# A deformable convolution's eviction issued behind the next band's first sample copy, and a second PSUM bank for split bands

## The chip, the cores and the metric

The kernel runs on one core of one Trainium2 chip. The time is device microseconds of one execution, here the median of several; lower is better. TensorE (PE) multiplies into PSUM[...]; ScalarE (ACT) and VectorE (DVE) read PSUM and write SBUF; GpSimd (POOL) and SyncE (SP) mostly issue transfers. Each engine works through its own instructions in order, and engines wait for one another by semaphores.

## The reference, cut to what matters

Input x has 8 images of 128 channels of 64 x 64 in fp32. Layer 0 is a group norm, a modulated deformable 3 x 3 convolution, a batch norm with ReLU, and the sum with x. Layer 1 is a group norm and a routed mixture of four 3 x 3 expert convolutions plus a shared one. The change lies in layer 0's deformable convolution:

```
om = conv3x3(x, off_w) + off_b            # 27 maps: y and x offsets, mask
off = om[:, :18].reshape(B, 9, 2, H, W);  mask = sigmoid(om[:, 18:])
py = off[:, :, 0] + rows + ky;  px = off[:, :, 1] + cols + kx
val = corner(y0, x0, (1 - ly) * (1 - lx)) + ... (four corners)
val = val * mask
out = einsum('bckhw,ock->bohw', val, w) + b
```

## The kernel before, in words

`dense()` computes layer 0 up to its statistics, with fp32 throughout; `layer1()` does the rest. Sampling is a product: for a tile of pixels, a matrix of bilinear weights (`s`, built by VectorE from the tables `x_wts` and `y_wts`, L868) is multiplied with the tile's input pixels (`xt`) on PE.

**Bands.** An image is eight bands of eight rows (`NB = 8`), 64 bands in all. The loop over g has 65 steps. Step g issues, in this order: for q = 0 to 4, `sample(5g+q)` (twelve PE products at L884 into one tile `pq`, then a ScalarE copy at L894 into `samples[g % 2]`) and `weights` of five groups later; behind q = 1, `put_off()`, which runs VectorE work set aside in `late`; and then `conv(g-1)`, the nine taps over the band before (L934, each tap two PE passes into `py`), with other work issued between the taps: the transposes of the pixels of band g+2 (L825 into `pt`, copied out at L828), the spreading and sharing of that band's tables (L776, L782, L841), loads (L738, L757), and pieces of the offset convolution of a later image (`tables`, L456 into `pc`). "The step j" below is the step whose samples are for the j-th band of an image, so that its convolution is for band j-1; the step j = 0 has the convolution of the last band of the image before.

**The convolution's output.** Behind its last tap, L942 evicts `py` with a bias into `y` on ScalarE, the batch norm's statistics of `y` go into `late` (L943, run at L1014), and L944 stores `y` from SP's queue. `py` has one bank (`ps_y`). A band covers 7 rows for j = 0 and 8 for j = 1 to 6; the last band of an image has two spans of 5 and 4 rows (320 and 256 columns), one behind the other in the same bank, each with its own nine taps, eviction and store.

**PSUM.** `ps_q` has three tiles of two banks (`pq`), so that the fourth group of a step waits for the copy of the first, and the fifth for that of the second. `ps_y` has one bank. `ps_c` has one bank under the tag `pc`, shared by the offset blocks and the transposes.

**What sets the order.** It is written out by hand: each engine runs its instructions in the order in which the Python code issues them (`manual_schedule`). The loads of tables go through POOL, the stores of `y`, of the offset maps and some copies through SP.

Of the kernel before, what the change touches and what calls it, by code (L numbers as in the profile page):

```python
# [8 lines left out]
F32 = mybir.dt.float32  # L9
I32 = mybir.dt.int32  # L10
AF = mybir.ActivationFunctionType
# [5 lines left out]
P = 128  # L17
# [5 lines left out]
CH = 512  # L23
# [42 lines left out]
def deform_moe_conv(  # L66
# [18 lines left out]
    nc = tc.nc  # L85
# [10 lines left out]
        out=gsel, in_=gsel, compare_op=ALU.is_ge, fill=0.0, base=0,  # L96
# [83 lines left out]
    def dense():  # L180

        with ExitStack() as st:
# [83 lines left out]
            count_f = a1.tile([1, 1], F32, name="count_f")  # L266

            nc.scalar.activation(count_f, nhalf[0:1], AF.Sigmoid)
            xts, ss, late = {}, {}, []
            bands = [(b, j) for b in range(B) for j in range(NB)]  # L270

            def pause(n):
# [527 lines left out]
            def pixels(g, turn_odd=False):  # L800

                if g >= len(bands):
                    return
                xts[g] = a2.tile([P, NCOL, P], F32, name="xt")
                if turn_odd:
                    for side in range(2):
                        nc.vector.tensor_copy(
                            picked_odd[:, :, :, T * side : T * side + T].rearrange(
                                "p c h x y -> p c h (x y)"
                            ),  # L810
                            picked[
                                :, 1 - side : EVEN - side, :, T * side : T * side + T
                            ].rearrange("p c h x y -> p c h (x y)"),
                        )
                for c0 in range(0, NCOL if turn_odd else EVEN, 4):
                    n = min(4, NCOL - c0)
                    if turn_odd:
                        pt = ps_q.tile([P, 2, CH], F32, name="pq")[:, 0].rearrange(
                            "p (c n) -> p c n", n=P
                        )  # L820
                    else:
                        pt = ps_c.tile([P, 4, P], F32, name="pt", tag="pc")
                    for c in range(c0, c0 + n):
                        one = picked[:, c] if c < EVEN else picked_odd[:, c - EVEN]
                        nc.tensor.transpose(  # L825
                            pt[:, c - c0], one.rearrange("p h x y -> p (h x y)"), ident
                        )
                    (nc.vector.tensor_copy if turn_odd else nc.scalar.copy)(  # L828
                        xts[g][:, c0 : c0 + n], pt[:, 0:n]
                    )  # L830
                    yield
# [90 lines left out]
            def conv(g):  # L922

                b, j = bands[g]
                o = 2 * T * j - 1
                spans = (
                    [(0, 7)] if j == 0 else [(o, 8)] if j < NB - 1 else [(o, 5), (o + 5, 4)]
                )
                for e, (o, n) in enumerate(spans):
                    py = ps_y.tile([P, CH], F32, name="py")[:, 0 : n * W]  # L930
                    for i in range(TAPS):
                        yy, xx = divmod(i, 3)
                        m = 3 * (o + 1 - yy - 2 * T * j + 2) + yy
                        nc.tensor.matmul(  # L934
                            py,
                            lhsT=dw_sb[:, 3 * (2 - yy) + 2 - xx],
                            rhs=samples[g % 2][:, m : m + 3 * n - 2 : 3, xx, 1 : W + 1],
                            start=(i == 0), stop=(i == TAPS - 1),
                        )
                        yield  # L940
                    y = a3.tile([P, CH], F32, name="y")[:, 0 : n * W]
                    nc.scalar.activation(y, py, AF.Identity, bias=db_sb)  # L942
                    late.append((nc.vector.bn_stats, ystats[:, b, j + e, :], y))  # L943
                    nc.sync.dma_start(out=ydram[b][:, o * W : (o + n) * W], in_=y)  # L944

            made, later = tables(0), tables(1)
            for q in range(4):
# [75 lines left out]
            for g in range(len(bands) + 1):  # L1023
                b, j = bands[g] if g < len(bands) else (B, 0)
                if j == NB - 4:
                    means_of = statistics(b + 2)
                turned = pixels(g + 2)
                if j == NB - 2:
                    tick()
                for q in range(NGR):  # L1030
                    if g < len(bands):
                        sample(g * NGR + q)
                        if g:
                            weights(g * NGR + q + AHEAD)
                        if g == 0 and q == 2:
                            for k in range(Q):
                                load_y(2, k, nc.gpsimd)
                    if g == 0 and q == 1:
                        for _ in range(4):
                            next(later)  # L1040
                    if q == 1:
                        put_off()
                taps = conv(g - 1) if g else iter(())
                twice = 2 if g and bands[g - 1][1] == NB - 1 else 1
                for done, _ in enumerate(taps):
                    part, odd = divmod(done, twice)
                    if odd == 0 and part in PIXELS:
                        next(turned, None)
                    if odd == 0 and part == 2:
                        load_x(g + 3, nc.gpsimd)  # L1050
                        if g < len(bands):
                            edges(g)
                    if odd == 0 and part > 6:
                        for k in range(T * (part - 7), T * (part - 6)):
                            load_y(g + 3, k, nc.gpsimd)
                    if odd == 0 and part in SPREAD:
                        step, half = divmod(SPREAD.index(part), 2)
                        if step:
                            spread(g + 2, HALVES[half], ())
                        else:  # L1060
                            spread(g + 2, sides_=(half,), clip=False)
                    if odd == 0 and part in SHARE:
                        piece = SHARE.index(part)
                        share(g + 2, piece, MOVES[piece])
                    if odd == 0 and j == NB - 4 and 0 < part < 7:
                        next(means_of, None)
                    if odd == 0 and j == NB - 3 and part == 0:
                        for _ in range(2):
                            next(means_of, None)
                    if odd == 0 and j == NB - 3 and part == 4 and b + 2 < B:  # L1070
                        for _ in made:
                            pass
                        asked, made = True, tables(b + 2)
                        next(made)
                    if odd == 0 and part in BLOCKS and asked:
                        asked = False
                        tick()
                    for _ in range(3 + (g < NB) if twice == 1 else 1 + done % 2):
                        tick()
                    if odd == 0 and part == 4:  # L1080
                        pick(g + 3)
                        if 2 <= j < 5:
                            load_quarter(b + 2, j - 1)
                    if odd == 0 and part == 8 and j == 1:
                        load_quarter(b + 2, 0)
                if g == 0:
                    edges(0)
                    spread(1)
                    for n in range(AHEAD):
                        weights(NGR + n)  # L1090
                for _ in turned:
                    pass
                if g == 0:
                    for piece in range(4):
                        share(2, piece, MOVES[piece])
                    load_x(3, nc.gpsimd)
                    for k in range(Q):
                        load_y(3, k, nc.gpsimd)
                    pick(3)
                    spread(2)  # L1100
                if g == 3:
                    quad_weights()
                if j < NB - 1 and g < len(bands):
                    late.append((hand_on, g))
                xts.pop(g - 1, None)
                if j == 1 and b:
                    nc.vector.bn_aggr(ymvs[:, b - 1], ystats[:, b - 1])
                if (b, j) == (B - 1, 1):
                    reach()
# [596 lines left out]
```

## Time and profile before

| | us |
|---|---|
| median of 3 runs (lowest to highest) | 1424.83 (1418.2 to 1427.55) |
| the profiled execution: its time, its span | 1419.31, 1417.3 |
| PE busy | 1290.2 (91%) |
| VectorE busy | 1063.5 (75%) |
| ScalarE busy | 834.3 (59%) |
| GpSimd busy | 477.6 (34%) |
| TensorE clock granted, mean | 0.967 of full |

A row of the profile gives source line, engine, operation, what is written and read, and how often, then busy time, mean ns of one, and the engine's idle time just ahead with what ended it. In a timeline a row begins with start and length; neighbouring instructions of one kind are merged into a row, with their number behind the x, and idle time ahead stands in brackets. Products on PE are pipelined, and their ends are modelled.

### The profile page before, as it was taken

How to read it: one execution, taken by the hardware profiler on the slowest of the kernel's cores; microseconds unless marked ns; L12 is line 12 of the kernel's file. 1: busy time of each engine (PE TensorE's matmuls, PEld its weight loads, DVE VectorE, ACT ScalarE, POOL GpSimd, SP SyncE). 2: the span in 40 equal slices, each digit the busy share in tenths (PEclk: the TensorE clock that was granted, in tenths of full speed). 3: DMA queues.
4: the chain of work that ended last, by engine and by line, in shares of the span. 5: the costliest groups of instructions: out<-in, count | busy, mean ns of one | idle time of the engine just before them, and what ended most of it. 6: DMA issues, size and time to landing. Idle time of an engine off the chain costs nothing.

```text
span 1417.3 us, 21259 instructions
## 1 busy us (share of the span) xinstructions
PE 1290.2 (91%) x7561; PEld 731.6 (52%) x7561; DVE 1063.5 (75%) x2124; ACT 834.3 (59%) x1110; POOL 477.6 (34%) x748
## 2 busy tenths in 40 slices
PE   4169889999999999999999999999948999999998
PEld 1144456555656655655565565666623444444443
DVE  5757868689788878968978886756448987778972
ACT  2365856886787688688679768767522333222220
POOL 6444044534425543452552554354021010001000
PEclk9579989999999999999999999999978999999999
DMA  4589686977978887897887887799245654456411
GB/s 145 114 192 206 137 182 157 213 182 171 210 181 180 194 195 175 180 207 184 193 210 183 179 207 159 159 228 220 66 160 147 163 146 123 127 153 178 104 57 51
DMA packets 149430, 234.55 MB, mean 165 GB/s; under 512 B 101677, under 2 KB 104890, under 8 KB 139074
## 3 DMA queue, kind: packets, MB, share of 16 engines
q0 software_dynamic: 79248, 136.19, 44.4%
q1 hardware_dynamic: 69522, 96.37, 24.2%
q8 instruction: 61, 1.00, 0.3%
q10 hardware_dynamic: 544, 0.54, 0.1%
q14 instruction: 55, 0.45, 0.1%
HBM read 180.23 MB, written 45.35 MB: 159 GB/s over the span
## 4 chain that ended last, share of the span: by engine, by line
PE 57%; DMA 12%; ACT 12%; issue 8%; DVE 6%; POOL 3%; SPq 2%; DVEq 0%; ACTq 0%; POOLq 0%
PE py L934 21%; PE pc L1618 17%; PE pq L884 11%; DMA ywts<-taby 3%; PE pc L456 3%; PE pt L825 3%; ACT xwts L776 2%; DMA combo<-colwise 2%; ACT work L638 2%; DMA pad<-in_x_dram 1%; ACT samples L894 1%; DMA x<-in_x_dram 1%; DVE s L868 1%; POOL ywts L738 1%; ACT xt L841 1%
## 5 line engine op out<-in xcount | busy, mean ns | idle before, releaser
L934 PE MATMUL py<-samples,dw_sb 128*128 128x512 f32 (+3 forms) x1296 | 555.1, 561 | 9.7 <-ACT y L942 9.7
L738 POOL DMA_DIRECT2D ywts<-taby x510 | 335.0, 671 | 368.0 <-DMA xwts<-tabx 151.8
L934 PEld LDWEIGHTS py<-samples,dw_sb 128*128 128x128 f32 x1296 | 226.8, 189 | 206.8 <-issue 174.2
L884 PE MATMUL pq<-s,xt 64*128 64x144 f32 (+1 forms) x3840 | 284.4, 302 | 29.8 <-ACT samples L894 22.5
L884 PEld LDWEIGHTS pq<-s,xt 64*128 64x128 f32 x3840 | 257.6, 191 | 78.6 <-ACT samples L894 26.9
L894 ACT COPY samples<-pq 128x864 f32<-128x864 f32 (+1 forms) x318 | 278.5, 973 | 27.2 <-PE pq L884 27.1
L868 DVE TENSOR_TENSOR s<-xwts,ywts 128x432 f32<-128x432 f32 (+1 forms) x448 | 199.0, 498 | 49.5 <-PE pq L884 45.4
L1618 PE MATMUL pc<-v,u 128*128 128x512 f32 x384 | 174.3, 600 | 6.3 <-DVE v L1525 6.3
L1618 PE MATMUL pc<-v,wmix 128*128 128x512 f32 x384 | 173.2, 596 | 0.0
L776 ACT ACTIVATE xwts<-xwts,place 128x1152 f32<-128x1152 f32 (+3 forms) x132 | 153.1, 1164 | 7.9 <-DMA xwts<-tabx 7.9
L782 DVE TENSOR_SCALAR xwts<-xwts 128x1152 f32<-128x1152 f32 (+2 forms) x128 | 96.0, 751 | 80.4 <-ACT xwts L776 75.3
L1596 ACT ACTIVATE t<-pc,bmix 128x512 f32<-128x512 f32 x32 | 22.0, 687 | 187.5 <-PE pc L1618 98.8
L757 POOL DMA_DIRECT2D xwts<-tabx x126 | 73.5, 590 | 164.3 <-DVE samples L911 34.9
L1618 PEld LDWEIGHTS pc<-v,u 128*128 128x128 f32 x384 | 71.8, 191 | 92.9 <-issue 83.1
L1618 PEld LDWEIGHTS pc<-v,wmix 128*128 128x128 f32 x384 | 72.0, 189 | 90.9 <-issue 88.9
L942 ACT ACTIVATE y<-py,db_sb 128x512 f32<-128x512 f32 (+3 forms) x72 | 45.8, 636 | 118.0 <-PE py L934 110.8
L828 ACT COPY xt<-pt 128x512 f32<-128x512 f32 x126 | 73.9, 587 | 61.0 <-PE pt L825 51.4
L825 PEld LDWEIGHTS pt<-ident,picked 128*128 128x128 f32 x504 | 59.0, 142 | 92.5 <-ACT xt L828 41.8
L825 PE MATMUL pt<-ident,picked 128*128 128x128 f32 x504 | 78.1, 278 | 23.5 <-DVE picked L791 17.0
L791 DVE COPY picked<-pad 128x512 f32<-128x512 f32 x128 | 71.9, 604 | 32.0 <-PE pt L825 31.9
L841 DVE COPY xt<-xt 32x896 f32<-32x896 f32 x126 | 77.7, 616 | 2.4 <-ACT xt L828 0.9
L1014 DVE BATCH_NORM_STATS2 ystats<-y 128x6 f32<-128x512 f32 (+3 forms) x72 | 44.2, 622 | 23.7 <-ACT y L942 23.7
(209 smaller groups left out, 1167.0 us busy)
## 6 DMA issues: line engine op xcount, KB each, us to landing
xwts<-tabx POOLq DMA_DIRECT2D x126, 576.0 KB, 8.5
pad<-in_x_dram SPq DMA_DIRECT2D x36, 512.0 KB
ywts<-taby POOLq DMA_DIRECT2D x126, 144.0 KB, 9.2
out_dram<-yo SPq DMA_DIRECT2D x32, 512.0 KB
ywts<-taby POOLq DMA_DIRECT2D x126, 108.0 KB, 8.9
yd<-y SPq DMA_DIRECT2D x48, 256.0 KB
ywts<-taby POOLq DMA_DIRECT2D x126, 72.0 KB, 8.3
pad<-yd SPq DMA_DIRECT2D x16, 512.0 KB
```

Of the source, the lines that this page charges most:

```text
L738: engine.dma_start(out=y_wts[g % 3][HALF * h + k : HALF * (h + n) : Q, first : last + 1].rearrange("p r a b c -> p (r a b c)"), in_=bass.A ...
L757: engine.dma_start(out=x_wts[g % 3][HALF * h : HALF * h + HALF], in_=bass.AP(tensor=x_table[b].tensor, offset=x_table[b].offset + (2 * j + ...
L776: nc.scalar.activation(some, some, AF.Abs, bias=columns[side])
L782: nc.vector.tensor_scalar(some, some, -1.0, 0.0, ALU.add, ALU.min)
L825: nc.tensor.transpose(pt[:, c - c0], one.rearrange("p h x y -> p (h x y)"), ident)
L828: (nc.vector.tensor_copy if turn_odd else nc.scalar.copy)(xts[g][:, c0 : c0 + n], pt[:, 0:n])
L841: move(out=xts[g][rows, EVEN:].rearrange("p c n -> p (c n)"), in_=xts[g][rows, 1 - side : EVEN - side].rearrange("p c n -> p (c n)"),)
L868: nc.vector.tensor_tensor(s[:, :, 3 * at : 3 * (at + k)].rearrange("p m (c x) -> p m c x", x=3), by_x[:, :, c : c + k], by_y[:, :, w : w + ...
L884: nc.tensor.matmul(by_m[:, h, :, at : at + k], lhsT=xts[g][rows, c // 2 + EVEN * (c % 2)], rhs=s[rows, :, at : at + k], start=True, stop=True,
L894: (nc.scalar.copy if g or q < 3 else nc.vector.tensor_copy)(bass.AP(tensor=one.tensor, offset=one.offset + first, ap=[list(one.ap[0]), [M ...
L934: nc.tensor.matmul(py, lhsT=dw_sb[:, 3 * (2 - yy) + 2 - xx], rhs=samples[g % 2][:, m : m + 3 * n - 2 : 3, xx, 1 : W + 1], start=(i == 0), ...
L1618: nc.tensor.matmul(pc, lhsT=us[j][:, kx], rhs=vs[g][:, rows, kx : kx + W], start=(kx == 0), stop=(kx == 2),)
```

## The change

Two edits of the convolution's output. First, the eviction with its statistics and its store is wrapped in a function `move`. For a band with one span it isn't run at once but put in the list `waiting`, and run in the next step of the loop behind `sample` of q = 0, that is behind the first sample copy in ScalarE's order (in the loop's last step, which has no samples, at its start). For a band with two spans it is run at once, as before. Second, the second span of such a band accumulates in the bank of `ps_c` instead of that of `ps_y`. The lists of instructions of the engines keep their lengths: on ScalarE each unsplit eviction stands one place later (in the steps j = 6 of the first images a normalisation also stands between), on VectorE its statistics follow the copy of four rows to the next band (L918, `hand_on`) instead of preceding it, and SP's order is unchanged.

```diff
@@ def conv(g)
                 for e, (o, n) in enumerate(spans):
-                    py = ps_y.tile([P, CH], F32, name="py")[:, 0 : n * W]
+                    if e == 0:
+                        py = ps_y.tile([P, CH], F32, name="py")[:, 0 : n * W]
+                    else:
+                        py = ps_c.tile([P, CH], F32, name="py2", tag="pc")[:, 0 : n * W]
...
-                    y = a3.tile([P, CH], F32, name="y")[:, 0 : n * W]
-                    nc.scalar.activation(y, py, AF.Identity, bias=db_sb)
-                    late.append((nc.vector.bn_stats, ystats[:, b, j + e, :], y))
-                    nc.sync.dma_start(out=ydram[b][:, o * W : (o + n) * W], in_=y)
+
+                    def move(e=e, o=o, n=n, py=py):
+                        y = a3.tile([P, CH], F32, name="y")[:, 0 : n * W]
+                        nc.scalar.activation(y, py, AF.Identity, bias=db_sb)
+                        late.append((nc.vector.bn_stats, ystats[:, b, j + e, :], y))
+                        nc.sync.dma_start(out=ydram[b][:, o * W : (o + n) * W], in_=y)
+
+                    if len(spans) > 1:
+                        move()
+                    else:
+                        waiting.append(move)
@@ the loop over g
                 turned = pixels(g + 2)
+                if g == len(bands) and waiting:
+                    waiting.pop()()
...
                     if g < len(bands):
                         sample(g * NGR + q)
+                        if waiting:
+                            waiting.pop()()
                         if g:
                             weights(g * NGR + q + AHEAD)
```

More of the change, by code (lines that the diff above doesn't have):

```diff
@@ L268, in dense @@
             nc.scalar.activation(count_f, nhalf[0:1], AF.Sigmoid)
-            xts, ss, late = {}, {}, []
+            xts, ss, late, waiting = {}, {}, [], []
             bands = [(b, j) for b in range(B) for j in range(NB)]
```

## The prediction

> **What bounds the kernel now.** I read the page's costliest groups first, then what TensorE (PE) waited for in one whole image, then busy time band by band, then the timeline of two bands. A band's step g runs five groups of sample products (L884), each copied out of PSUM by ScalarE (L894), and then the nine taps of the convolution of band g-1 (L934), evicted by L942. The page first:
>
> ```profile
> L934 PE MATMUL py<-samples,dw_sb 128*128 128x512 f32 (+3 forms) x1296 | 555.1, 561 | 9.7 <-ACT y L942 9.7
> L894 ACT COPY samples<-pq 128x864 f32<-128x864 f32 (+1 forms) x318 | 278.5, 973 | 27.2 <-PE pq L884 27.1
> L942 ACT ACTIVATE y<-py,db_sb 128x512 f32<-128x512 f32 (+3 forms) x72 | 45.8, 636 | 118.0 <-PE py L934 110.8
> ```
>
> ScalarE waits 110.8 us in all for the convolution to end: where it does, the eviction lies in an idle hole. PE waits 9.7 us for that eviction. PE's waits within one image (step 456.26 to 574.56), then its steps with the bands j = 3, 4 and 5 (columns: length, then busy us of PE, PE's loads, DVE, ACT):
>
> ```profile
> PE pq L884 <- ACT samples L894: 1.7, 2, 1.2
> PE py L934 <- ACT y L942: 0.9, 1, 0.9
> ...
> 502.70:515.82 13.12, 13.12 (x88) 7.88 (x87) 8.41 (x21) 11.33 (x16) 6.54 (x10) 1.00 1.07 213
> 515.82:529.78 13.96, 13.44 (x87) 7.97 (x87) 12.61 (x27) 13.45 (x19) 1.26 (x2) 1.00 0.74 187
> 529.78:544.87 15.09, 13.88 (x91) 8.42 (x91) 14.92 (x33) 11.59 (x16) 1.34 (x2) 1.00 0.79 180
> ```
>
> PE is busy in all of j = 3 at full clock; only j = 4 and 5 hold it up for ScalarE's copies, and j = 0 for the eviction. So PE's order of work is the time, and a stall added to a full band is added to the span. The timeline of the start of j = 3 (ScalarE ahead), of j = 4 (ScalarE behind), and of the end of j = 0's step:
>
> ```profile
> 502.70 4.21 PE L884 MATMUL pq<-s,xt 64*128 64x216 f32 x60
> 502.80 0.69 ACT L942 ACTIVATE y<-py,db_sb 128x512 f32<-128x512 f32 x1 [2.11 <-PE py L934]
> 503.87 4.40 ACT L894 COPY samples<-pq 128x1008 f32<-128x1008 f32 x5 [0.38 <-PE pq L884]
> 504.81 0.91 ACT L894 COPY samples<-pq 128x864 f32<-128x864 f32 x1
> ...
> 517.30 0.67 ACT L942 ACTIVATE y<-py,db_sb 128x512 f32<-128x512 f32 x1
> 517.87 4.31 ACT L894 COPY samples<-pq 128x1008 f32<-128x1008 f32 x5
> 518.94 1.94 PE L884 MATMUL pq<-s,xt 64*128 64x144 f32 x24 [0.52 <-ACT samples L894]
> ...
> 589.95 0.94 ACT L841 COPY xt<-xt 32x896 f32<-32x896 f32 x1
> 590.91 0.53 ACT L942 ACTIVATE y<-py,db_sb 128x320 f32<-128x320 f32 x1
> 591.49 4.22 PE L934 MATMUL py<-samples,dw_sb 128*128 128x256 f32 x18 [0.93 <-ACT y L942]
> ```
>
> In j = 3 the eviction runs from 502.80 to 503.49, while PE makes the first group; the first copy can't start before 503.87 anyway. It is free there. In j = 4 it is what the first copy waits for.
>
> **Part 1: the eviction behind the first copy.** Nothing is removed; 55 of the 72 evictions move (the sixteen of the split bands don't, and the last unsplit one has no copy to move behind). The products write three buffers of two banks, so group 4 waits for copy 1 and group 5 for copy 2. From the single records of j = 3, the groups start at 502.70, 503.66, 504.40, 505.13 and 505.87, and copy 2 ends at 504.81 + 0.91 = 505.72: 0.15 us before group 5 wants its buffer. With the move, copy 1 stays at 503.87, the eviction takes the place at 504.81, and copy 2 shifts by what an eviction takes from its start to the next start: 517.87 - 517.30 = 0.57. Copy 2 then ends at 506.29, group 5 starts 0.57 - 0.15 = 0.42 late, plus 0.02 to 0.09 to set off again (in j = 4 copy 1 is 0.88 later than in j = 3, measured from the step's start, with slack of 0.21 and 0.15 before groups 4 and 5, and the five groups take 0.84 longer). I take 0.48. Behind group 5 everything on PE is the same order: the transposes' copy (xt, 508.46) would find ScalarE free at 508.74, and PE's own delay puts it at 508.94, so nothing is added twice. ScalarE itself gives the 0.57 back in the hole before the next eviction would have run, which is now empty.
>
> The Trainium skill ("ScalarE: Activation LUTs", section "What ACT_TABLE_LOAD costs") prices an activation with a bias pointer at 280 ns + 0.833 ns an element, with 93 ns of overlap: 0.61 for 512 columns, where the trace has 0.57. By the page the stall would be 0.52 and the sum below 1.5 us more; I keep the trace.
>
> How often: by ScalarE's idle time ahead of copy 1, 35 steps are like j = 3 (j = 0, 2, 3, 6, more in the first image and all in the last), eight of them with a 448-wide eviction, 0.05 shorter. Two others of the first image (steps 6 and 8, where the eviction also ran before a later wait) pay about 0.5. In 18 steps ScalarE is behind (j = 4, 5, 7): there copy 1 goes 0.57 earlier, group 4 with it, but copy 2 has the same two instructions ahead of it as before and ends where it did, so group 5 starts where it did: nothing, and 0.1 lost in three of them, in which copy 1 would wait 0.15 for its product. Seven steps (j = 1) keep the old order, since their eviction is that of a split band. Sum: 27 x 0.48 + 8 x 0.43 + 2 x 0.5 + 0.3 = 17.7 us. Not seen in the trace is whether the shifted copy costs more or less than this; bounds 0.35 (PE finds part of it in its load queue) and 0.57 (no slack at all): 13 to 21.
>
> What is queued behind: on VectorE the statistics of y now follow the four-row hand-on. In j = 3 they ran at 505.14 and the hand-on at 505.74; swapped, the statistics come at 505.68 and y ends at 505.50: no wait, with 0.18 to spare, and VectorE has 4.7 us idle in that step. In j = 0, where VectorE is busy 20.56 of 21.08 us, it comes to the statistics more than 7 us after y. Cost nothing; were that cover gone, up to 0.2 us a step, on an engine not at its limit in those steps. The eviction's store on SP keeps its place in SP's order and is up to 2 us later; in j = 2 and 3 SP reached it only at 497.24 and 510.54, 7 us after y, in the others the transfer behind it starts 5 us later or more. Nothing on POOL moves past it. The next taps need the bank at 506.84, and it is free at 505.50.
>
> **Part 2: the second span's bank.** In a band that is an image's last, the second nine taps no longer wait for the first span's eviction. The stall to be removed is one per image; single records: 2.17, five of 0.93, 1.39 and 0.62, together 8.8. Ends of products are modelled 0.16 us after the point at which the next could start (taps of 320 columns follow one another every 0.28 and last 0.44), so 8 x 0.16 = 1.3 comes on top: 10.1 us. The new bank is the one of the offset blocks; its last reader in j = 0 ends at 589.92 and PE is through with the first span at 590.4, so no wait replaces it, and no offset product or transpose lies between the 18 products of the second span in PE's order. The next user, the transposes of j = 1, come 5 us after the second eviction. PE then reaches the sample products of j = 1 about 1.1 us sooner; their weights lie ready since 587, ScalarE has been idle for 2.42 and VectorE for 1.34 before them, so the gain holds. Bounds: 8.2 (part lost to VectorE, busy till 595.46) and 10.6.
> The rule against my figure: the skill ("Perfetto Trace Analysis", section "Optimizing Tensor Performance", on matmuls) says that groups rotated through different banks hide the eviction. That would be worth the eviction alone, 8 x 0.55 = 4.4 us; the trace shows more, because ScalarE is in the 0.94 us copy of L841 when the taps end and the eviction queues behind it.
>
> **Sum.** +17.7 - 10.1 = +7.6 us. The profiled execution took 1419.3 us (span 1417.3), so it becomes 1426.9. The median of the three runs is 1424.83, 5.5 above it; with the same step it becomes 1432.4, and I say 1432.
>
> **Rivals.**
> - Faster: the steps where ScalarE is behind gain. If group 5 didn't wait on copy 2 but only group 4 on copy 1, the 18 steps would win some 0.55 each, 10 us, the full bands would lose nothing, and with part 2 the kernel would gain 20 (1405); if the groups only half overlap, some 5 to 10 (1415 to 1420). It decides at the start of group 5 in j = 4: earlier than before, or not. For it: the first copy does go earlier. Against it: PE's 1.94 us for groups 4 and 5 in j = 4 holds a second small hold-up at copy 2. Chance 0.12, of which 0.05 passes 1%.
> - Slower: in the steps behind, copy 1 doesn't move up (the copy finds its product late) while copy 2 still shifts. Price 18 x 0.5 = 9 more, or the later chain (transposes' copy, L776) adds the 0.57 again in the full bands, 35 x 0.3 = 10: +17 to +27, 1442 to 1452. It decides where product 1 is ready later than ScalarE is free; in j = 4 it is ready at 517.0 and ScalarE at 517.30. Chance 0.16.
> - Part 2 does nothing, since the block's bank is still held: then +17.7, 1442. Its last reader is 0.5 us clear of the need, so this is counted within the slower cases.
>
> **How the numbers follow.** My forecast has 0.72; its bounds are 13 - 10.6 to 21 - 8.2, +2 to +13, or 1427 to 1438. The three runs alone lie 9 us apart, so about 1% (14 us) is what a measurement of this kernel can tell from no change. That range alone leaves out 0.28, so it is carried into the faster rival's milder half (to 1418, 0.04 of the 0.12) and the lower end of the slower one (to 1443, 0.04 of the 0.16): 1418 to 1443. Faster by over 1%: 0.05; slower by over 1%: 0.15, nearly all of the slower rival; within 1%: 0.80.
>
> **What would show it.** Right: group 5 in the j = 3 steps waits about 0.45 for L894 and those steps last 13.6 instead of 13.12; PE's waits for L894 grow from 22.5 us by some 12 to 18; j = 4 and 5 keep 13.96 and 15.09; the eviction's wait ahead of the 256-column taps is gone and j = 0's step is shorter by about 0.6 net. Wrong: no new wait at L894, or a shorter step in j = 4 and 5 (the faster rival); a wait of VectorE for y, or steps of j = 4, 5 and 7 grown by half a microsecond (the slower).

## The result and the profile after

The changed kernel takes 1432.88 us (median of 6 runs, 1432.59 to 1434.4); on the same chip the kernel before took 1421.79 (6 runs, 1418.2 to 1427.55). The ratio is 1.0079, with a 95% interval of 1.0061 to 1.0097: 11.1 us slower. Executions more than 1.5% above the fastest of their kernel count as slow and stay out of the ratios below. The profiled execution took 1432.98 us with a span of 1430.9, 13.7 more than that of before, at a granted clock of 0.969 against 0.967, so the clock explains none of it.

First the row of the sample products on the page of before, then the costliest groups of the page of after; L937 and L947 are the former L934 and L942:

```profile
L884 PE MATMUL pq<-s,xt 64*128 64x144 f32 (+1 forms) x3840 | 284.4, 302 | 29.8 <-ACT samples L894 22.5
```

```profile
L937 PE MATMUL py<-samples,dw_sb 128*128 128x512 f32 (+3 forms) x1296 | 553.8, 561 | 0.8 <-ACT y L947 0.8
...
L894 ACT COPY samples<-pq 128x864 f32<-128x864 f32 (+1 forms) x318 | 283.6, 970 | 129.7 <-PE pq L884 129.7
L884 PE MATMUL pq<-s,xt 64*128 64x144 f32 (+1 forms) x3840 | 294.3, 302 | 44.6 <-ACT samples L894 37.7
...
L947 ACT ACTIVATE y<-py,db_sb 128x512 f32<-128x512 f32 (+3 forms) x72 | 45.9, 638 | 27.2 <-PE py L937 26.1
```

PE no longer waits for the eviction (9.7 us before, 0.8 now), but its waits for the sample copies are 37.7 us where they were 22.5. (The 0.8 that is left is the wait of the last split band for the unsplit eviction ahead of it.) On ScalarE the idle time ahead of the eviction fell from 118.0 to 27.2 and that ahead of the copies rose from 27.2 to 129.7: the eviction left its idle hole, and the hole now stands empty ahead of the first copy.

Busy time by step (length, then busy us of PE, PE's loads, DVE, ACT, POOL; clock; DMA share; GB/s): a step j = 0 of before, then the steps j = 0, 3, 4 and 5 of the same image in after:

```profile
456.26:477.34 21.08, 20.15 (x201) 14.00 (x201) 20.56 (x38) 13.16 (x17) 13.03 (x19) 1.00 0.82 186
...
461.69:482.14 20.45, 20.14 (x201) 14.13 (x200) 18.79 (x36) 13.05 (x17) 9.38 (x15) 1.00 0.85 191
508.15:521.97 13.82, 13.38 (x87) 7.92 (x87) 8.54 (x21) 11.30 (x16) 5.62 (x9) 1.00 1.05 201
521.97:535.92 13.95, 13.59 (x87) 7.97 (x86) 12.62 (x27) 13.45 (x19) 1.18 (x2) 1.00 0.74 180
535.92:551.02 15.10, 14.09 (x91) 8.42 (x90) 14.91 (x33) 11.61 (x16) 1.45 (x2) 1.00 0.78 180
```

The step j = 3 went from 13.12 to 13.82 us; j = 4 and 5 kept 13.96 and 15.09 within 0.01. A step j = 0 was 21.08 and is 20.45. And the timeline of the two kinds of step in after, PE and ScalarE in order of time:

```profile
508.15 3.34 PE L884 MATMUL pq<-s,xt 64*128 64x216 f32 x48
509.33 1.04 ACT L894 COPY samples<-pq 128x1008 f32<-128x1008 f32 x1 [3.17 <-PE pq L884]
510.39 0.69 ACT L947 ACTIVATE y<-py,db_sb 128x512 f32<-128x512 f32 x1
510.98 3.43 ACT L894 COPY samples<-pq 128x864 f32<-128x864 f32 x4
511.93 1.13 PE L884 MATMUL pq<-s,xt 64*128 64x144 f32 x12 [0.45 <-ACT samples L894]
...
523.45 1.01 ACT L894 COPY samples<-pq 128x1008 f32<-128x1008 f32 x1
524.36 0.67 ACT L947 ACTIVATE y<-py,db_sb 128x512 f32<-128x512 f32 x1
524.94 3.39 ACT L894 COPY samples<-pq 128x864 f32<-128x864 f32 x4
525.88 1.13 PE L884 MATMUL pq<-s,xt 64*128 64x144 f32 x12 [0.36 <-ACT samples L894]
```

In both, group 5 (the row of twelve products) now stands alone behind a wait for the second copy. In j = 4 it starts 3.91 us into the step with the step's length unchanged; in j = 3 it starts at 3.78, where 505.87 - 502.70 = 3.17 was its place before. The two steps differ in one more thing: at 510.39 the eviction starts 0.02 behind the end of the copy (509.33 + 1.04), at 524.36 it starts 0.10 before it (523.45 + 1.01).

Summed over the 65 steps, after less before: 28 full steps other than j = 0 +18.9, seven steps j = 0 -5.9, step 6 +1.0, the steps behind -0.2, the first two +0.3, all from the last step with samples on -0.5; together 13.5 of the 13.7.

### The profile page after: what moved, and what is told of

Its sections match the earlier page's. It is cut to its first block, busy times and chain, and to the rows that moved or that the text cites. A ratio compares the mean times of both kernels' runs of the same rounds, so it can differ in the third digit from the quotient of the medians.

```text
span 1430.9 us, 21207 instructions
## 1 busy us (share of the span) xinstructions
PE 1298.6 (91%) x7561; PEld 733.1 (51%) x7561; DVE 1066.8 (75%) x2124; ACT 833.7 (58%) x1110; POOL 465.1 (33%) x748
## 4 chain that ended last, share of the span: by engine, by line
PE 60%; ACT 15%; DMA 9%; issue 7%; DVE 4%; SPq 2%; POOL 2%; ACTq 0%; DVEq 0%; POOLq 0%
PE py L937 27%; PE pc L1632 15%; PE pq L884 9%; ACT samples L894 6%; PE pc L456 3%; PE pt L825 3%; ACT y L947 2%; DMA x<-in_x_dram 2%; ACT xwts L776 2%; ACT work L638 2%; DMA ywts<-taby 1%; DMA combo<-colwise 1%; SPq L554 1%; ACT work L642 1%; DMA tabx<-combo 1%
## 5 line engine op out<-in xcount | busy, mean ns | idle before, releaser
L937 PE MATMUL py<-samples,dw_sb 128*128 128x512 f32 (+3 forms) x1296 | 553.8, 561 | 0.8 <-ACT y L947 0.8
L738 POOL DMA_DIRECT2D ywts<-taby x510 | 324.0, 652 | 368.7 <-DMA xwts<-tabx 158.4
L894 ACT COPY samples<-pq 128x864 f32<-128x864 f32 (+1 forms) x318 | 283.6, 970 | 129.7 <-PE pq L884 129.7
L884 PE MATMUL pq<-s,xt 64*128 64x144 f32 (+1 forms) x3840 | 294.3, 302 | 44.6 <-ACT samples L894 37.7
L937 PEld LDWEIGHTS py<-samples,dw_sb 128*128 128x128 f32 x1296 | 227.8, 189 | 195.2 <-issue 173.7
L776 ACT ACTIVATE xwts<-xwts,place 128x1152 f32<-128x1152 f32 (+3 forms) x132 | 153.2, 1164 | 7.8 <-DMA xwts<-tabx 7.8
L782 DVE TENSOR_SCALAR xwts<-xwts 128x1152 f32<-128x1152 f32 (+2 forms) x128 | 95.9, 750 | 81.1 <-ACT xwts L776 75.9
L828 ACT COPY xt<-pt 128x512 f32<-128x512 f32 x126 | 73.9, 586 | 62.0 <-PE pt L825 52.4
L841 DVE COPY xt<-xt 32x896 f32<-32x896 f32 x126 | 77.4, 614 | 2.5 <-ACT xt L828 0.9
L947 ACT ACTIVATE y<-py,db_sb 128x512 f32<-128x512 f32 (+3 forms) x72 | 45.9, 638 | 27.2 <-PE py L937 26.1
L841 ACT COPY xt<-xt 32x896 f32<-32x896 f32 x63 | 59.1, 938 | 1.5
```

The source lines that it names most:

```text
L738: engine.dma_start(out=y_wts[g % 3][HALF * h + k : HALF * (h + n) : Q, first : last + 1].rearrange("p r a b c -> p (r a b c)"), in_=bass.A ...
L776: nc.scalar.activation(some, some, AF.Abs, bias=columns[side])
L782: nc.vector.tensor_scalar(some, some, -1.0, 0.0, ALU.add, ALU.min)
L828: (nc.vector.tensor_copy if turn_odd else nc.scalar.copy)(xts[g][:, c0 : c0 + n], pt[:, 0:n])
L841: move(out=xts[g][rows, EVEN:].rearrange("p c n -> p (c n)"), in_=xts[g][rows, 1 - side : EVEN - side].rearrange("p c n -> p (c n)"),)
L884: nc.tensor.matmul(by_m[:, h, :, at : at + k], lhsT=xts[g][rows, c // 2 + EVEN * (c % 2)], rhs=s[rows, :, at : at + k], start=True, stop=True,
```

## Experiments

Ratios are against the kernel before on the same chip. "Part 1" is the moved eviction, "part 2" the second bank; an experiment is a change of the kernel after unless its diff is against before.

### Each part alone

The kernel before with the moves of the change and both spans in `ps_y`:

```diff
@@ part 1 alone, against after
-                    if e == 0:
-                        py = ps_y.tile([P, CH], F32, name="py")[:, 0 : n * W]
-                    else:
-                        py = ps_c.tile([P, CH], F32, name="py2", tag="pc")[:, 0 : n * W]
+                    py = ps_y.tile([P, CH], F32, name="py")[:, 0 : n * W]
```

> The change's first part alone: evictions behind the first sample copy, both spans of a split band in one bank as before. Theory (the fifth group waits for the second copy, and the bank's gain is a separate term): about 10 us above the changed kernel, that is 20 to 24 us above the kernel before (ratio 1.014 to 1.017); full steps last 13.8 us, as in the changed kernel, and PE's wait for the eviction of the split bands is back at 9 to 10 us. Rival (the second bank was worth nothing, and its wait has only moved): the same time as the changed kernel, 11 us above the kernel before.

Measured: 1444.73 us, ratio 1.016 (1.0138 to 1.0182), +22.6. The steps j = 0 and 3 of the image shown above, in this run:

```profile
467.71:489.36 21.65, 20.41 (x201) 14.07 (x200) 19.79 (x37) 13.05 (x17) 12.16 (x20) 1.00 0.89 207
515.36:529.18 13.82, 13.38 (x87) 7.92 (x86) 8.54 (x20) 11.13 (x16) 5.57 (x10) 1.00 1.05 209
```

The step j = 3 lasts 13.82 as in after; five of the seven steps j = 0 are 0.56 or 0.57 longer than before.

The kernel before with the second bank only, the evictions where they were (a bank is the piece of PSUM that `py` takes, 512 fp32 values in each partition):

```diff
@@ part 2 alone, against before
-                    py = ps_y.tile([P, CH], F32, name="py")[:, 0 : n * W]
+                    if e == 0:
+                        py = ps_y.tile([P, CH], F32, name="py")[:, 0 : n * W]
+                    else:
+                        py = ps_c.tile([P, CH], F32, name="py2", tag="pc")[:, 0 : n * W]
```

> The second part alone: the second span of a split band in the other bank, evictions where they were. Theory: 9 to 11 us below the kernel before (ratio 0.992 to 0.994), full steps at 13.12 us, no wait of PE ahead of the 256-column taps. Rival (the gain is given back in the next step, to VectorE or to the loads): within 3 us of the kernel before.

Measured: 1413.65 us, ratio 0.9937 (0.9913 to 0.9961), -8.5. The step j = 0, by windows of this run:

```profile
340.70:360.59 19.89, 19.89 (x202) 14.09 (x201) 19.43 (x37) 13.15 (x17) 9.95 (x16) 1.00 0.70 161
```

PE is busy in all 19.89 us; before, the step had 21.08. Five steps j = 0 are 1.19 or 1.20 shorter, and the seven together 10.07; the eighth split band, behind the last samples, gains 0.9 more. The full steps have 13.12 again. So the two parts add up in the steps: +0.57 and -1.19 in j = 0 give the -0.62 of after. By time +22.6 - 8.5 = +14.1 stands beside the measured +11.1, which their intervals (several us each) allow.

In its profiled execution one step of part 2 alone is much longer than before, step 12 (20.48 us for 15.74), and PE's timeline there tells why:

```profile
276.37 0.88 PE L884 MATMUL pq<-s,xt 64*128 64x216 f32 x6
282.58 5.37 PE L884 MATMUL pq<-s,xt 64*128 64x144 f32 x54 [5.33 <-DMA xt<-xt]
```

PE waits 5.33 us for the pixels that SP shares (L841). SP's queue in the same run and then in before, at the place where that transfer is issued:

```profile
257.37 12.39 SPq L554 DMA_DIRECT2D combo<-colwise  x5
269.81 1.83 SPq L281 DMA_DIRECT2D pad<-in_x_dram  x1
271.74 0.37 SPq L947 DMA_DIRECT2D yd<-y  x1
272.22 0.61 SPq L841 DMA_DIRECT2D xt<-xt  x1
```

```profile
253.47 5.83 SPq L554 DMA_DIRECT2D combo<-colwise  x5
259.34 0.53 SPq L281 DMA_DIRECT2D pad<-in_x_dram  x1
259.97 0.50 SPq L944 DMA_DIRECT2D yd<-y  x1
260.60 0.61 SPq L841 DMA_DIRECT2D xt<-xt  x1
```

Five loads of the column table held SP for 12.39 us instead of 5.83, and the transfer, fourth in line, was issued at 272.22 instead of 260.60. The longer step takes back 4.7 us in that execution, and the same wait stands in step 12 in the profiles of three of the kernels below. Why the loads took longer was not found.

### The eviction one or two copies later

If copy 2 is what costs, the eviction behind it should cost less: group 5 then finds its buffer as before.

```diff
@@ the eviction behind the second copy
-                        if waiting:
+                        if waiting and q == 1:
                             waiting.pop()()
```

> The changed kernel with the eviction behind the second sample copy instead of the first. Theory (what costs is that the second copy, for which the fifth group waits, comes late): the fifth group no longer waits; the third to fifth copies are still late by 0.6 to 0.7 us, so the copy of the first transposes is 0.3 to 0.4 late and with it PE's second transposes: full steps of 13.4 to 13.5 us instead of 13.8, and 8 to 12 us less than the changed kernel, so within 3 us of the kernel before. Rival (the cost is ScalarE's displaced 0.6 to 0.7 us wherever it stands): 13.8 us a step and the time of the changed kernel.

Measured: 1420.08 us, ratio 0.9994 (0.9979 to 1.001). Windows and timeline of the same two bands in this run:

```profile
505.65:519.16 13.51, 13.31 (x87) 7.87 (x86) 8.49 (x21) 11.19 (x16) 6.55 (x10) 1.00 1.03 220
519.16:532.78 13.62, 13.59 (x87) 7.98 (x87) 12.63 (x27) 13.36 (x19) 1.27 (x2) 1.00 0.74 192
```

```profile
505.65 4.20 PE L884 MATMUL pq<-s,xt 64*128 64x216 f32 x60
506.83 1.84 ACT L894 COPY samples<-pq 128x1008 f32<-128x1008 f32 x2 [3.18 <-PE pq L884]
508.70 0.69 ACT L947 ACTIVATE y<-py,db_sb 128x512 f32<-128x512 f32 x1
509.28 2.63 ACT L894 COPY samples<-pq 128x864 f32<-128x864 f32 x3
511.77 0.62 ACT L828 COPY xt<-pt 128x512 f32<-128x512 f32 x1
512.44 0.66 PE L825 MATMUL pt<-ident,picked 128*128 128x128 f32 x4 [0.20 <-ACT xt L828]
```

The sixty sample products are one row of 4.20 us again, without a wait. But the delay only moves on: the transposes' copy (L828) finds no idle time ahead of it, where after has 0.20, and the second transposes wait for it. The step lasts 13.51, still 0.39 more than before. In j = 4 and 5, though, copy 1 and copy 2 are both early now, and these steps became 0.34 shorter (13.62 here), which the expectation did not have: the faster rival's gain exists, but two copies are needed for it.

```diff
@@ the eviction behind the third copy
-                        if waiting:
+                        if waiting and q == 2:
                             waiting.pop()()
...
-                    if q == 1:
+                    if q == 1 or q == 2:
                         put_off()
```

> The changed kernel with the eviction behind the third sample copy, and its statistics run a group later as well. Theory: no group of products waits, but the next taps write the same bank and begin 4.1 us into the step, while the eviction ends at 4.4 to 4.6; so the taps wait 0.3 to 0.5 us for the eviction (a wait of PE for it in every full step, which no earlier place has), and the first transposes' copy is as late as behind the second: full steps of 13.5 to 13.6 us, the time 0 to 4 us above the kernel with the eviction behind the second copy. Rival (only the order within ScalarE's copies counts): 13.5 and no wait of the taps.

Measured: 1421.51 us, ratio 1.0012 (1.0001 to 1.0023). PE and ScalarE in j = 3 of this run:

```profile
506.65 0.69 ACT L947 ACTIVATE y<-py,db_sb 128x512 f32<-128x512 f32 x1
507.24 1.84 ACT L894 COPY samples<-pq 128x864 f32<-128x864 f32 x2
507.39 1.15 PE L937 MATMUL py<-samples,dw_sb 128*128 128x512 f32 x2 [0.39 <-ACT y L947]
```

Here the bank itself is late: the next band's taps stand behind the eviction, in 55 places and for 18.1 us in the whole run. The step lasts 13.58. So in a full step no place behind the first, second or third copy is free; each place delays another buffer, and costs 0.70, 0.39 and 0.46 us a step.

### Why the eviction starts late in the full steps

In the full steps the last work of ScalarE ahead of the copies is its own sharing copy of 32 partitions (L841). Three runs put something else there, and one changed its kind.

```diff
@@ ScalarE's sharing copy two taps earlier, SP's transfer two taps later
-            SHARE = 6, 4, 8, 2
+            SHARE = 6, 2, 8, 4
```

> The changed kernel with ScalarE's part of the pixel sharing (the copy of 32 partitions) issued two taps earlier, ahead of the second spreading activation, and SP's part two taps later, so that this copy is no longer ScalarE's last work of a step. Theory (in the full steps the eviction starts only behind the end of the first copy, 0.13 us later than in the steps where the sharing copy isn't the last work, and that makes 0.13 of the 0.70 us a step): the eviction starts 0.1 us ahead of the first copy's end, full steps last 13.7 us instead of 13.8, the time is 3 to 4 us below the changed kernel. Rival (the missing overlap has another cause, such as the eviction's own wait): steps of 13.8 us and the same time as the changed kernel within 1 us.

Measured: 1450.29 us, ratio 1.0202 (1.0174 to 1.023). The full steps fell to 13.69, and the eviction there overlaps the copy (512.12 for a copy end of 512.23); but the steps j = 4, 5 and 7 grew to 15.03, 15.60 and 17.7, and two of the steps j = 4 to 20.45 and 19.49 with PE waiting 4.8 and 4.2 us for SP's transfer of pixels. The next run took the part of SP out, and moved ScalarE's copy alone:

```diff
@@ ScalarE's sharing copy alone two taps earlier
-            SHARE = 6, 4, 8, 2
+            SHARE = 6, 2, 8, 2
...
-                    if odd == 0 and part in SHARE:
-                        piece = SHARE.index(part)
-                        share(g + 2, piece, MOVES[piece])
+                    for piece in (3, 1, 0, 2):
+                        if odd == 0 and part == SHARE[piece]:
+                            share(g + 2, piece, MOVES[piece])
```

> The changed kernel with ScalarE's part of the pixel sharing two taps earlier, as in the run that was 17 us above the changed kernel, but with SP's part left where it was. Theory (there SP's transfer came to stand behind the column loads in SP's queue and landed late for the steps j = 4, 5 and 7; the earlier ScalarE copy itself does no harm): steps j = 4, 5 and 7 back at 13.95, 15.1 and 16.7, full steps at 13.69, and 3 to 4 us below the changed kernel, about 1429, ratio 1.004 to 1.007. Rival (moving ScalarE's copy is what lengthened those steps): they stay at 15.0, 15.6 and 17.7.

Measured: 1448.5 us, ratio 1.0208 (1.019 to 1.0225). The two steps of about 20 us are gone from the profile, but the 15.03 stays and the median fell by no more than 1.8, so my theory fell and the rival holds. ScalarE's timeline of this run, at the end of j = 3:

```profile
519.73 0.94 ACT L841 COPY xt<-xt 32x896 f32<-32x896 f32 x1
520.68 1.14 ACT L776 ACTIVATE xwts<-xwts,place 128x1008 f32<-128x1008 f32 x1
523.09 1.20 ACT L660 ACTIVATE combo<-combo 64x576 f32<-64x576 f32 x3 [1.28 <-DVE combo L613]
```

With the copy ahead of it, L776 comes later; in after ScalarE stood idle 0.31 ahead of L660, here 1.28. VectorE clips the output of L776 (L782) and stands in order ahead of L613, for which ScalarE then waits; the tents and the first copy of j = 4 come behind that. The step j = 4 is 1.07 us longer for it.

```diff
@@ ScalarE's sharing copy as an activation
+            def act_copy(out, in_):
+                nc.scalar.activation(out, in_, AF.Identity)
+
             MOVES = (
-                nc.vector.tensor_copy, nc.scalar.copy, nc.vector.tensor_copy, nc.sync.dma_start
+                nc.vector.tensor_copy, act_copy, nc.vector.tensor_copy, nc.sync.dma_start
```

> The changed kernel with ScalarE's sharing copy made an activation with the function Identity in its old place, as the last work of a step. If it is the kind of instruction (a copy, two copies ahead of an activation) that keeps the eviction from overlapping with the first sample copy, the eviction now starts 0.1 us ahead of that copy's end and full steps last 13.7 us; if it is what that instruction does (32 partitions, its wait for ScalarE's own earlier copies), they stay at 13.8.

Measured in one execution: 1432.91 us, full steps 13.83. The kind of instruction is not the cause. Last, the copy was left where it is and a small activation set behind it:

```diff
@@ one element a partition behind the sharing copy
                         share(g + 2, piece, MOVES[piece])
+                        if piece == 1:
+                            nc.scalar.activation(scratch, db_sb, AF.Identity)
```

> The changed kernel with one more instruction on ScalarE behind its 32-partition copy at L841: an activation of one element on each of 128 partitions, so that the 32-partition copy is no longer ScalarE's last work before the next step's first sample copy. Theory: it is the 32-partition copy standing last that makes the eviction start 0.03 us behind the end of the copy ahead of it instead of 0.10 before it. Then in the full steps the eviction overlaps again and those steps last 13.69 us instead of 13.82, as they did with the copy put two taps earlier; the steps j = 4 and 5, where ScalarE is behind, lengthen by the price of the instruction, 0.1 to 0.3 us. Rival: what counts is which instruction is ahead of the copies in another way (the second L776 behind the copy, say) and the eviction stays 0.03 behind, with 13.82 in the full steps.

Measured in one execution: 1429.02 us beside 1421.59 for before. ScalarE at the start and at the end of j = 3, in this run (lines of the source stand one further down):

```profile
507.77 1.04 ACT L895 COPY samples<-pq 128x1008 f32<-128x1008 f32 x1 [2.96 <-PE pq L885]
508.71 0.68 ACT L948 ACTIVATE y<-py,db_sb 128x512 f32<-128x512 f32 x1
509.29 3.43 ACT L895 COPY samples<-pq 128x864 f32<-128x864 f32 x4
...
517.35 0.94 ACT L842 COPY xt<-xt 32x896 f32<-32x896 f32 x1
518.30 0.20 ACT L1081 ACTIVATE scratch<-db_sb 128x1 f32<-128x1 f32 x1
```

The eviction starts 0.10 before the copy's end, and the full step lasts 13.69. An added instruction of 0.20 us made 34 steps 0.11 to 0.14 shorter than in after, and five steps j = 5 0.1 longer.

The traces say more exactly what the 32-partition copy does: the first activation behind it starts without overlap, however many copies over 128 partitions lie between. In after, 34 of the moved evictions are that first activation, and 33 of them start 0.02 or 0.03 behind the end of the copy ahead; the other 21 have some other activation between, and all overlap by about 0.10. With the small activation in place it is this one that starts 0.01 behind the end (517.35 + 0.94 and 518.30), and all 55 evictions overlap. Why the first activation loses it, by the 32 partitions or by something else in that copy, is not shown.

### Looking for a better version

Part 2 alone gains, and the eviction behind the second copy gains in the steps behind. The first attempt to join them:

```diff
@@ part 2, and the eviction behind the second copy in chosen steps
-                    if len(spans) > 1:
+                    if len(spans) > 1 or j not in (3, 4) or not 0 < b < B - 1:
...
-                        if waiting:
+                        if waiting and q == 1:
```

> The second part, and the eviction moved only in the steps j = 4 and 5 of the second to seventh image (where ScalarE is behind PE), there behind the second sample copy; everywhere else it stays where the kernel before has it. Theory (behind the second copy the fourth and fifth group both start earlier there, which took those steps from 13.96 to 13.62 and from 15.09 to 14.76 with all evictions moved so, while the full steps lose nothing when the eviction stays in its hole): twelve steps shorter by 0.34 on top of the second part alone, 4 us less than it, about 1409 to 1410, ratio 0.989 to 0.992. Rival (those steps are set by ScalarE's total work, and the 0.34 came from the longer steps before them, in which ScalarE got ahead): within 1 us of the second part alone, steps of 13.96 and 15.09.

Measured: 1415.9 us, ratio 0.9967 (0.9955 to 0.9978). The `j` of this line is that of the convolution's band, whose eviction runs two steps later, so the evictions of the steps j = 5 and 6 were moved, not of 4 and 5: step 37 (j = 5) has 14.77 and gained 0.32, step 38 (j = 6) lost 0.40; one step j = 5, step 29, grew to 15.81. With `(2, 3)` in place of `(3, 4)`:

> The second part, and the eviction behind the second sample copy in the steps j = 4 and 5 of the second to seventh image alone (the run before that was meant to do so moved it in the steps 5 and 6 instead: step 5 fell to 14.77 and step 6 rose to 13.52). Theory (behind the second copy the fourth and fifth group both start earlier, by what ScalarE stood idle ahead of the transposes' copy): steps of 13.62 and 14.76, 4 us less than the second part alone by the sum of the steps, ratio to the kernel before 0.989 to 0.992; an execution in which PE waits for SP's pixel transfer in step 12 is 4 to 6 us above that. Rival (what ScalarE gains in step 4 is paid in step 5, or to that transfer in every execution): the time of the second part alone, ratio 0.993 to 0.995.

Measured: 1413.12 us, ratio 0.9937 (0.9923 to 0.9951), no different from part 2 alone. Most of the chosen steps are 13.62 and 14.75 long as expected, but the four steps j = 7 behind them are 0.41 to 0.60 longer than in part 2 alone, and step 12 lasts 22.63 us with a wait of 7.35 for SP's pixels. This wait could go if ScalarE issued that transfer itself:

```diff
@@ part 2 alone, the transfer issued by ScalarE
-                nc.vector.tensor_copy, nc.scalar.copy, nc.vector.tensor_copy, nc.sync.dma_start
+                nc.vector.tensor_copy, nc.scalar.copy, nc.vector.tensor_copy, nc.scalar.dma_start
```

> The second part, and the fourth piece of the pixel sharing (a transfer of 32 partitions) issued from ScalarE's queue instead of SP's, at the same place in the program. Theory (what stretches step 12 by 4 to 6 us in some executions, and makes the times of the second part range over 9 us, is that this transfer stands behind the slow column loads in SP's queue): no wait of PE for it in step 12, a range of the times of 4 us or less, and a median at the low end of the second part alone, 1408 to 1411. Rival (the transfer is late because of what the 16 transfer engines carry at that time, not because of the queue it is issued from): the wait and the range stay.

Measured: 1451.03 us, ratio 1.019 (1.0156 to 1.0225). The wait in step 12 is gone (15.75 us), but five other steps are 5 to 10 us longer, and the times spread over 16 us. ScalarE's timeline ahead of one of them, in this run:

```profile
393.41 0.40 ACT L779 ACTIVATE xwts<-xwts,place 128x144 f32<-128x144 f32 x1
402.74 0.51 ACTq L841 DMA_DIRECT2D xt<-xt  x1
403.30 1.14 ACT L776 ACTIVATE xwts<-xwts,place 128x1008 f32<-128x1008 f32 x1 [9.49 <-DMA pad<-in_x_dram]
```

The issue of the transfer waits for an earlier one, a load of the input that SP issued (`pad<-in_x_dram`): in the trace both signal on the same semaphore, and ScalarE's queue stands until that load has landed. All of ScalarE's work now stands behind it, 9.49 us with the issue itself. The two changes together:

> Both edits together: the second part, evictions behind the second copy in the steps j = 4 and 5, and the pixel transfer from ScalarE's queue. Theory (they act on different waits): 3 to 4 us less than with the transfer alone, about 1405 to 1407, ratio 0.988 to 0.991. Rival (ScalarE is the limit in the steps j = 4 and 5, and issuing costs it what the order saved): the same as the transfer alone.

Measured: 1443.71 us over 14 executions, from 1421.95 to 1457.27. The ratio, 1.0078 (1.0051 to 1.0104), is of the seven fastest alone, with a median of 1431.58. The profile has the short steps of the one (13.62 to 13.73 and 14.76) and the stalls of the other (5.9, 7.2, 8.3 and 2.1 us). No version was faster than part 2 alone, about 8 us under before.

## Why the prediction held, and where its sum was off

**The time.** Predicted 1432, range 1418 to 1443; measured 1432.88. The agreement within 1 us is luck: the step from before to after was put at +7.6 and is +11.1 in the medians and +13.7 between the profiled executions. The base made up for it, since the median of before, 1424.83 from three runs, became 1421.79 with six.

**Part 1 in the full steps: right mechanism, size off.** The chain was the one named: eviction, copy 2, group 5, and no second delay behind it, since the transposes' copy still has its 0.20 of idle time. PE's waits for L894 grew by 15.2 us (expected 12 to 18). The step grew by 0.70, not 0.48. The term that failed is the 0.57 for the eviction's place in front of copy 2, which was read in j = 4, where the eviction overlaps the copy ahead. From the start of copy 1 to the start of copy 2 it is 510.98 - 509.33 = 1.65 in j = 3 of after and 524.94 - 523.45 = 1.49 in j = 4; in j = 3 of before it was 504.81 - 503.87 = 0.94. So copy 2 is 0.71 later, not 0.57: 0.13 of that is the overlap lost behind the 32-partition copy, which the runs with that copy elsewhere (13.69) and with the small activation behind it (13.69) give back. The second term too small is PE's new start, put at 0.02 to 0.09: group 5 starts 0.05 behind the end of copy 2 and then takes 0.09 longer than in before. With both, 0.71 - 0.15 + 0.05 + 0.09 = 0.70, as measured. The steps j = 0, which keep the overlap, show the new start alone: 0.57 where 0.48 was predicted. The bound "no slack at all, 0.57" was therefore no bound. The sum of 17.7 came out as 22.6 by part 1 alone (19.6 to 25.9 by the interval). The rule weighed there, an estimate of 0.61 for an activation of 512 columns from start to start by the Trainium skill ("ScalarE: Activation LUTs", "What ACT_TABLE_LOAD costs"), against the trace's 0.57: after has 0.59 from the eviction's start to copy 2's in j = 3 and 0.58 in j = 4, between the two and nearer to the trace.

**Part 1 elsewhere: right.** The steps j = 4 and 5 kept their lengths in the images where ScalarE is behind, and j = 7 grew by 0.06 to 0.13 in three images, as expected. A fourth was 0.40 shorter, 16.72 for 17.11; it is 16.72 with either part alone as well, so the one long step lies in the profiled execution of before and not in the change. Neither rival's mechanism showed: the steps behind gained nothing (it takes the second copy ahead as well, as the run with it shows, for 0.34 a step), and they lost nothing.

**Part 2: right, and a little too small.** 10.1 was predicted for eight stalls; 10.07 is what the seven steps j = 0 gave, and the eighth band 0.9 more, so about 11 stands beside an upper bound of 10.6. The term left out is again PE's new start: in before the second product behind a stall comes 0.10 later than it does without one, eight times. By time the part gives 8.5 (5.5 to 12.4 by the interval), with one step 4.7 us longer in its profiled execution for a transfer on SP that no view of before showed. Read as the eviction alone, the Trainium skill's rule of rotating banks ("Perfetto Trace Analysis", "Optimizing Tensor Performance") would have had 4.4 of it; the trace's wait, with the share copy in front of the eviction, was the right measure.

## What to carry to other kernels

An eviction that sits in an idle hole of its engine may be free only there: moved in among copies that free buffers, it delays those behind it, and the wait comes back at whatever is then freed late. Here that was the ring of the sample products behind the first copy, the transposes' tile behind the second, and its own bank behind the third. Before a shift is priced, the distance from start to start is read in a step of the same kind as those it is charged to, not in one where the engine was behind. Of two edits that go together, each is worth its own sum: here one gained 8.5 us and the other lost 22.6.

## What the runs showed of the hardware

- A moved eviction on ScalarE starts about 0.10 us before the end of the copy ahead of it, unless it is the first activation behind a copy over 32 partitions: then it starts 0.02 or 0.03 behind the end (33 of 34 in after), with one, two or three copies over 128 partitions between. An activation of 128 x 1 elements (0.20 us) put behind the 32-partition copy restored the overlap, and 0.13 us a step with it.
- Issuing a transfer from ScalarE's queue held ScalarE for 9.49 us in one place: the issue waited for an earlier transfer to land, and the engine's computing stood behind it.
- Five loads of a column table took SP 5.83 us to issue in one run and 12.39 in another, and the transfer behind them was then 5 us late for PE. The times of part 2 alone scatter over 9 us where those of after scatter over 2. Whether this wait makes the scatter is open: before scatters over 9 us too, and its profile has no such wait.
